# Order of VectorE's work in layer 0, PSUM banks in layer 1 and a longer lag in layer 2 of a four-layer graph attention kernel

## The chip, the core and the metric

The kernel runs on one core of a Trainium2 chip. The core has five engines that run at the same time, each with a queue of its own: TensorE (PE in the profile: matrix products and transposes), VectorE (DVE), ScalarE (ACT), GpSimd (POOL, here the issuer of all indirect gathers) and SyncE (SP, here an issuer of plain transfers). They wait for one another through semaphores. Products land in PSUM, which the kernel allocates in banks of 128 partitions by 512 floats; whoever wants a bank again waits until its last reader is done. The metric is the device time of one execution in microseconds; the median of three is taken.

## What is computed

A node matrix `x` (4096 x 256) passes four graph attention layers over one adjacency matrix `adj` (4096 x 4096, about nine neighbours a node, with the diagonal). Every layer normalises, clips at zero and adds its output to `x`:

```
h = maximum(layernorm(x), 0);  x = x + layer(h, adj)

layer 0: h = x @ W.T in 8 heads; logits = leaky(e_l[i] + e_r[j]) + gate * (|curv[i] - curv[j]| @ Wc.T)
         softmax over the neighbours j; out = attn @ h
layer 1: h = x @ W.T; e = leaky(a1.h[i] + a2.h[j]); out = softmax(e) @ h
layer 2: the same kind of e; out = elu(concat(softmax(e) @ x, -softmax(-e) @ x) @ wtrans)
layer 3: 4 heads; h = x @ W.T + b; score = leaky(h[i].h[j]), 1.0 where there is no edge
         out = relu(softmax(score) @ h)
```

Since the matrix is sparse, the kernel turns it into lists of edges first and then works on these.

## The kernel before

**Tiles and chunks.** The nodes are cut into 32 tiles of 128 rows (`NT`). The edges of a tile are packed into nine chunks (`EC`) of 128. For each chunk GpSimd issues one indirect DMA (L914) that fetches the rows of the neighbours from a table in device memory into a buffer `g`; there are six such buffers (`G`). The first seven chunks need rows below 3584 of the table only (28 tiles of 32); the last two may need any row. In layers 1 and 3 the ninth chunk is not gathered but expanded on TensorE (L1688, a product of a comparison matrix `to` with the table's last rows) and copied into `g` by ScalarE (L1692). That makes 9, 8, 9 and 8 gathers a tile in layers 0 to 3, 1088 in all.

**Who orders what.** TensorE runs in the order in which the program names its instructions (`manual_schedule`). The other engines' queues are ordered by a scheduler. `tc.issue_after(ins)` makes it put an instruction behind another of the same engine. `behind` is a dictionary of instructions to stand behind: `scores`, used in layers 1 and 2, puts its first addition (L1760) behind all that it holds.

**Layer 0** reads `adj`, finds each row's neighbours and works on the tiles, all at once. Its steps are put into a list `plan`, each with a due time in the plan's own units, and the program names them in the order of those times. Finding: `piece` and `pack` make keys (L1225), `rank` (L1229) picks the largest keys of a row with `nc.vector.max` (L1240) and `match_replace` (L1242), `columns` turns them into column numbers, `places` (L1365, its last operation at L1415) gives every edge its place, both for four tiles at once; `mark` (L897, L901) and `find_edges` make the numbers `nbr` (L1466) that the gathers take. Attention: `begin0` issues the gathers, `before0` (L1498, L1512) prepares, `score0` (L1505: `d`, the difference of the curvatures, then `e`), `turn_d`, `curve`, `weigh0` (L1531 multiplies the gathered rows by the weights), `attend0`, `finish0`, `turn1` and `rows1`, which makes the table of layer 1. The tile's work is centred on a time `w`, 22 units after its gathers are due; `score0` stands at `w - 9`. Tiles follow one another every 11.5 units.

**Layers 1 to 3** are driven by `run`. It takes a list of steps, each with a lag: in round r the step is called for tile r minus lag, and within a round steps are called in the order of the list. So in layer 1 TensorE meets, in round r: `go_to` of tile r+3 (L1674, a broadcast of column numbers that VectorE compares at L1677), `give2` of r-3, `attend1` of r-1, `turn2` of r-2, `before1` of r+1 (`give`, and the transposes of `s_chunks`), `rows2` of r-2 and `expand1` of r+1. `give` multiplies nine chunks into three small columns each (L908), which VectorE sums (L1752). Banks: `go_to` and `expand1` take turns in the one bank "pe" of the pool `ps_e`; `give` and `give2` in the one bank "pm" of `ps_m`.

In layer 2 the order on TensorE is `attend2` of r (L1894, 28 products), `turn3` of r-2 (L863, the transposes of the normed row `r`, L843), `turn_signed` of r-1 (L1916), `rows3` of r-2 (L872, which makes layer 3's table), `before2` of r+1 (L1641) and `through_wt` of r-1 (L1929). `finish2` (from L1937 on) makes `r` from the result of `through_wt`. Layer 3's first gathers wait until the rows of tile 27 are in its table.

Of the kernel before, what the change touches and what calls it, by code (L numbers as in the profile page):

```python
# [20 lines left out]
P = 128  # L21
C = 256
KC = C // P
H0, D0, CF = 8, 32, 6
# [672 lines left out]
EC = 9  # L697
# [16 lines left out]
def gnn_lists(  # L714
# [27 lines left out]
    nc = tc.nc  # L742
    N = x_in.shape[0]
    NT = N // P
# [77 lines left out]
    own = [const.tile([P, NT, 3], F32, name=f"own{i}") for i in (1, 2)]  # L822
# [8 lines left out]
    behind = {}  # L831
# [23 lines left out]
    def bank(pool, name, dtype=F32):  # L855
        t = pool.tile([P, 512], F32, name=name)
        return t if dtype == F32 else t.bitcast(dtype)
# [96 lines left out]
    with tc.tile_pool(name="keep", bufs=1) as keep, tc.tile_pool(  # L954
# [9 lines left out]
        g = g_pool.tile([P, EC + 1, ROW0], F32, name="g").rearrange("p c k -> p (c k)")  # L964
# [44 lines left out]
        for i, size in enumerate((0.5, 1.0)):  # L1009
            d = keep.tile([P, P], BF16, name=f"off_diag{i}")  # L1010
# [41 lines left out]
        at = keep.tile([P, NT], F32, name="at")  # L1052
# [176 lines left out]
        def rank(t):  # L1229

            r, i = divmod(t, RG // P)
            src = bank(ps_t, "pt")[:, : NH * KP]
            for h in range(NH):
                nc.tensor.transpose(
                    src[:, h * KP : (h + 1) * KP], key_t[r, h][:KP, i * P : (i + 1) * P], ident[:KP, :KP]
                )
            left = find.tile([P, NH * KP], F32, name="left", bufs=1)
            for a in range(0, KMAX, 8):
                best = keys[:, t, a : a + 8]
                nc.vector.max(out=best, in_=src)  # L1240
                if a + 8 < KMAX:
                    nc.vector.match_replace(out=left, in_to_replace=best, in_values=src, imm_value=-1.0)  # L1242
                    src = left
# [65 lines left out]
        lists = {}  # L1309
# [54 lines left out]
        def places(q, n):  # L1364


            s = slice(q, q + n)
            K = KMAX + KX
            is_, lasts, both = lists.pop(q)
            ps = bank(ps_t, "pt")[:, : 4 * n].rearrange("p (a t) -> p a t", a=4)  # L1370
            nc.tensor.matmul(ps[:, 0, :], lhsT=below, rhs=degree[:, s, 0], start=True, stop=True)
            nc.tensor.matmul(ps[:, 1, :], lhsT=up_to, rhs=degree[:, s, 1], start=True, stop=True)
            for i in range(2):
                nc.tensor.matmul(ps[:, 2 + i, :], lhsT=ones, rhs=degree[:, s, i], start=True, stop=True)

            def tmp(name, *shape):
                return find.tile([P, GT, *shape], F32, name=name, bufs=1)[:, :n]


            end, first, step = tmp("end"), tmp("first", 2), tmp("step", 2)  # L1380
            nc.vector.tensor_scalar(end, ps[:, 3, :], -1.0, float(HALF), op0=OP.mult, op1=OP.add)
            nc.vector.tensor_scalar(
                end, end, float(LATE * P - HALF), second, op0=OP.min, op1=OP.mult
            )
            nc.vector.scalar_tensor_tensor(
                at[:, s], ps[:, 0, :], room, end, op0=OP.add, op1=OP.add
            )
            nc.vector.tensor_scalar(at_late[:, s], ps[:, 1, :], float(HALF), None, op0=OP.add)
            nc.scalar.copy(of_tile[:, s, :], ps[:, 2:, :].rearrange("p a t -> p t a"))
            for i, a in enumerate((at, at_late)):  # L1390
                nc.vector.scalar_tensor_tensor(
                    minus[:, s, i], a[:, s], -2.0, degree[:, s, i], op0=OP.mult, op1=OP.subtract
                )


            nc.vector.tensor_sub(first[:, :, 0], at[:, s], lasts[:, :, 1])
            nc.vector.tensor_sub(step[:, :, 0], at_late[:, s], first[:, :, 0])
            nc.vector.tensor_sub(step[:, :, 1], lasts[:, :, 0], degree[:, s, 1])
            nc.vector.tensor_add(first[:, :, 1], at[:, s], step[:, :, 1])
            nc.vector.tensor_sub(step[:, :, 1], at_late[:, s], first[:, :, 1])  # L1400
            nc.vector.tensor_add(step[:, :, 1], step[:, :, 1], lasts[:, :, 1])
            place_, late = tmp("place_", K), is_[:, :, 1, :]
            for i, (a, b) in enumerate(((0, KMAX), (KMAX, K))):
                shape = [P, n, b - a]
                nc.vector.tensor_tensor(
                    late[:, :, a:b], late[:, :, a:b], step[:, :, i : i + 1].to_broadcast(shape),
                    op=OP.mult,
                )
                nc.vector.tensor_tensor(
                    place_[:, :, a:b], first[:, :, i : i + 1].to_broadcast(shape),  # L1410
                    slot[:, None, a:b].to_broadcast(shape), op=OP.add,
                )
            nc.vector.tensor_add(place_, place_, late)

            nc.vector.scalar_tensor_tensor(  # L1415
                both[:, :, 0, :], is_[:, :, 0, :], float(FAR), place_, op0=OP.mult, op1=OP.add
            )
            for i in range(n):
                of0[q + i]["list"] = both[:, i]

        def fits():

# [78 lines left out]
        def score0(t):  # L1501
            g = of0[t]["g"]
            pe = of0[t]["b"][:, : (EC + 1) * V0].rearrange("p (c k) -> p c k", c=EC + 1)
            d = of0[t]["d"] = work.tile([P, EC, CF], F32, name="d")
            nc.vector.tensor_sub(d, g[:, :EC, C + H0 :], pe[:, :EC, H0:])  # L1505
            e = of0[t]["e"] = work.tile([P, EC + 1, H0], F32, name="e")
            nc.vector.tensor_add(e, g[:, :, C : C + H0], pe[:, :, :H0])
            nc.vector.scalar_tensor_tensor(e, e, 0.2, e, op0=OP.mult, op1=OP.max)
# [65 lines left out]
        def at_piece(i):  # L1574
            return 8 + T_PIECE * min(i, FIRST) + T_LATER * max(i - FIRST, 0)
# [15 lines left out]
        for q, n in groups:  # L1591
            for t in range(q, q + n):
                last = at_piece((t // (RG // P) + 1) * per_r - 1) + 7 + 2.5 * (t % (RG // P))
# [6 lines left out]
        begun = {}  # L1600
# [3 lines left out]
            put(when, mark, t)  # L1604
            put(when + 4, find_edges, t)
        for t in range(NT):
            w = begun[t] + 22
            put(begun[t], begin0, t)
            put(max(begun[t] + 0.1, begun[0] + 12), begin0_late, t)
            put(w - 10, before0, t)  # L1610
            put(w - 9 + 0, score0, t)
            put(w - 7.8 + 0, turn_d, t)
            put(w + 2, curve, t)
            put(w + 3, weigh0, t)
            put(w + 15, attend0, t)
            put(w + 20, finish0, t)
            put(w + 24.6, turn1, t)
            put(w + 27, rows1, t)
        put(found[NT - 1] + 20, fits)
        for _, _, f, a in sorted(plan, key=lambda p: p[:2]):  # L1620
            f(*a)
        bad_1 = const.tile([P, 1], F32, name="bad_1")
        nc.vector.tensor_reduce(bad_1, bad, AX.X, OP.add)


    with tc.tile_pool(name="work", bufs=2) as work, tc.tile_pool(name="kept", bufs=1) as kept, tc.tile_pool(
# [36 lines left out]
        def keep_late(rows, width):  # L1663

            for b in range(0, LB, 2):
# [2 lines left out]
                rest = work.tile([P, 2, ROW1], F32, name="rest", bufs=1)[:, :n, :width]  # L1668
                in_parts([late_rows[:, b : b + n, i, :width] for i in range(3)], row, rest)

        def go_to(t, to):

            pm = bank(ps_e, "pe")[:, :P]
            nc.tensor.matmul(  # L1674
                pm, lhsT=col_late[:, t : t + 1].to_broadcast([P, P]), rhs=ident, start=True, stop=True
            )
            nc.vector.tensor_tensor(  # L1677
                to.rearrange("p (b e) -> p b e", b=LB), pm[:, None, :].to_broadcast([P, LB, P]),
                late_no[:, :, None].to_broadcast([P, LB, P]), op=OP.is_equal,
            )  # L1680
# [64 lines left out]

        a2_of = kept.tile([P, NT, EC + 1], F32, name="a2_of")

        def give(a, st, own_t):

            pe = bank(ps_m, "pm")[:, : EC * 3]  # L1750
            to_edges(pe.rearrange("p (c s) -> p c s", c=EC), st, upper(own_t))
            nc.vector.tensor_reduce(a[:, :EC], pe.rearrange("p (c s) -> p c s", c=EC), AX.X, OP.add)  # L1752
            nc.scalar.copy(a[:, SELF:], own_t[:, 0:1])
# [10 lines left out]
        with tc.tile_pool(name="l1_o", bufs=2, space=PSUM) as ps_o, tc.tile_pool(  # L1764
# [11 lines left out]

            def before1(t, of):
                a = of["a"] = work.tile([P, EC + 1], F32, name="a")
                give(a, of["st"], own[0][:, t, :])
                of["s"] = s_chunks(of["st"])  # L1780

            def give2(t, of):
                give(a2_of[:, t, :], of.pop("st"), own[1][:, t, :])

            def weigh1(t, of):
                s = scores(of["g"], of.pop("a"))
# [62 lines left out]
        with tc.tile_pool(name="l2_o", bufs=1, space=PSUM) as ps_o, tc.tile_pool(  # L1849
# [93 lines left out]

            rows3_of = []

            def turn3(t, of):
                of["hT"] = transposed(work, ps_t, of.pop("r"))

            def rows3(t, of):
# [19 lines left out]
                for k in range(K3):  # L1969
# [4 lines left out]
            run(  # L1974
                table2, ROW1, xs[1],
                [
                    (0, weigh2), (1, signed2), (2, finish2), (0, attend2), (2, turn3), (1, turn_signed),
                    (2, rows3), (-1, before2), (1, through_wt),
                ],
            )  # L1980

# [213 lines left out]
```

## Time and profile before

The time before is 1615.28 us, the median of three runs from 1614.99 to 1616.41. The execution that the profiler recorded is longer, 2272.3 us; all times below are of that one.

| stage | stretch, us | rounds | what bounds are in sight |
|---|---|---|---|
| up to the first gather | 0 to 108.4 | | reading `adj`, first lists |
| gathers of layer 0 | 108.4 to 753.6 | 32 tiles x 9 | |
| gathers of layer 1 | 780.1 to 1259.7 | 32 x 8 | TensorE busy 250.55 of 420 us |
| gathers of layer 2 | 1281.0 to 1724.3 | 32 x 9 | TensorE busy 349.52 of 440 us |
| gathers of layer 3 | 1766.3 to 2206.1 | 32 x 8 | TensorE busy 296.81 of 400 us |
| end | 2206.1 to 2272.3 | | last tiles |

The profile's page has a row of busy times by engine, then groups of equal instructions: engine, operation, output and input, how many, and behind the bar their busy time, the mean of one in ns, and how long the engine stood idle just before them, with the releaser of most of it. A line of the timeline reads: start, duration, engine, source line, operation, output and input, and in brackets the idle time before it and what ended it. A line of waits reads: who waited for whom, total us, times, longest. "issue" and "remote" name no instruction: the profile shows nothing, or something that it can't tell, as the releaser. The end of a product on TensorE is modelled.

### The profile page before, as it was taken

How to read it: one execution, taken by the hardware profiler on the slowest of the kernel's cores; microseconds unless marked ns; L12 is line 12 of the kernel's file. 1: busy time of each engine (PE TensorE's matmuls, PEld its weight loads, DVE VectorE, ACT ScalarE, POOL GpSimd, SP SyncE). 2: the span in 40 equal slices, each digit the busy share in tenths (PEclk: the TensorE clock that was granted, in tenths of full speed). 3: DMA queues.
4: the chain of work that ended last, by engine and by line, in shares of the span. 5: the costliest groups of instructions: out<-in, count | busy, mean ns of one | idle time of the engine just before them, and what ended most of it. 6: DMA issues, size and time to landing. Idle time of an engine off the chain costs nothing.

```text
span 2272.3 us, 28902 instructions
## 1 busy us (share of the span) xinstructions
PE 1431.2 (63%) x9569; PEld 1013.5 (45%) x9584; DVE 1100.3 (48%) x2979; ACT 765.2 (34%) x2246; POOL 1054.0 (46%) x1145
## 2 busy tenths in 40 slices
PE   5723745656646726656556637878889367767776
PEld 3412423333434414434444425666667345445544
DVE  5724635555543524434333323554555256666666
ACT  4623624454222322222222102333334143343343
POOL 2154243443344354454444455666562635565550
PEclk9855766666666857777777858999999778898888
DMA  8855555665333354444444444555554444455530
GB/s 284 267 187 172 187 172 180 212 212 163 83 88 99 88 164 130 128 124 129 130 133 131 140 138 122 158 161 157 155 156 139 129 134 147 149 157 154 161 107 21
DMA packets 167341, 338.02 MB, mean 149 GB/s; under 512 B 31760, under 2 KB 103696, under 8 KB 167184
## 3 DMA queue, kind: packets, MB, share of 16 engines
q0 software_dynamic: 52224, 145.30, 24.5%
q1 hardware_dynamic: 67714, 134.54, 18.1%
q10 hardware_dynamic: 47246, 56.27, 7.1%
q8 instruction: 77, 1.26, 0.2%
q14 instruction: 80, 0.66, 0.1%
HBM read 282.22 MB, written 53.77 MB: 148 GB/s over the span
## 4 chain that ended last, share of the span: by engine, by line
PE 25%; issue 12%; DVE 9%; another core or an unknown queue 8%; ACT 3%; POOL 1%; DMA 1%; DVEq 0%; ACTq 0%; POOLq 0%
PE o L934 5%; PE o L1894 4%; PE o L939 4%; PE pv L2025 3%; PE pt L872 3%; DVE v L2031 2%; PE pt L1929 2%; PE o L943 1%; POOL g L914 1%; DVE s L2052 1%; PE s_ps L1641 1%; DMA g<-table,nbr 1%; PE pe L1674 1%; DVE g L2064 1%
## 5 line engine op out<-in xcount | busy, mean ns | idle before, releaser
L914 POOL DMA_INDIRECT g<-table,nbr x1088 | 1037.8, 954 | 1065.1 <-issue 433.9
L1894 PE MATMUL o<-g,sw 128*128 128x257 f32 x896 | 206.0, 388 | 31.2 <-DVE sw L1872 23.6
L1894 PEld LDWEIGHTS o<-g,sw 128*128 128x128 f32 x896 | 173.1, 194 | 59.7 <-issue 25.3
L863 PE MATMUL pt<-ident,r 128*128 128x128 f32 x256 | 61.9, 328 | 193.4 <-DVE r L843 60.4
L2025 PE MATMUL pv<-parts,st 64*128 64x256 bf16 (+1 forms) x864 | 106.3, 308 | 97.8 <-DVE v L2031 42.0
L2031 DVE TENSOR_TENSOR v<-pv,g 128x512 f32<-128x512 f32 (+1 forms) x160 | 97.3, 634 | 89.6 <-remote 51.2
L863 PEld LDWEIGHTS pt<-ident,r 128*128 128x128 f32 x256 | 34.4, 162 | 219.2 <-issue 115.4
L1192 ACT ACTIVATE mask<-adj,minus_half 128x1024 bf16<-128x1024 int32 x112 | 125.2, 1141 | 18.1 <-issue 6.8
L934 PE MATMUL o<-g,sw 128*128 128x257 f32 (+1 forms) x320 | 125.5, 544 | 0.0
L865 ACT COPY hT<-pt 128x256 f32<-128x256 f32 x128 | 46.9, 367 | 233.4 <-PE pt L863 144.3
L872 PE MATMUL pt<-wcat,hT 128*128 128x272 f32 (+2 forms) x384 | 96.7, 371 | 45.3 <-ACT hT L865 32.4
L1674 PE MATMUL pe<-ident,col_late 128*128 128x128 f32 x64 | 23.3, 463 | 158.2 <-issue 144.8
L2025 PEld LDWEIGHTS <-st 64*128 64x128 bf16 (+1 forms) x864 | 61.4, 104 | 136.6 <-issue 125.9
L2081 ACT ACTIVATE y<-o,inv 128x64 f32<-128x64 f32 x128 | 36.0, 312 | 243.4 <-DVE inv L2077 143.5
L939 PE MATMUL o<-g,sw 128*64 128x257 f32 (+1 forms) x768 | 117.3, 448 | 0.0
L896 ACT ACTIVATE off<-place,minus 128x1152 bf16<-128x1152 f16 x64 | 80.0, 1250 | 58.1 <-DVE st L897 53.0
L1505 DVE TENSOR_TENSOR d<-g,pb 128x54 f32<-128x54 f32 x32 | 6.8, 211 | 180.1 <-remote 124.9
L934 PEld LDWEIGHTS o<-g,sw 128*128 128x128 f32 x320 | 85.8, 279 | 18.1 <-DVE g L2064 0.3
L872 PEld LDWEIGHTS pt<-wcat,hT 128*128 128x128 f32 x384 | 66.1, 208 | 60.2 <-ACT hT L865 36.5
L1531 DVE TENSOR_TENSOR g<-g,pb 128x2560 f32<-128x2560 f32 x32 | 90.1, 2816 | 4.7 <-ACT pb L1528 4.4
L1674 PEld LDWEIGHTS pe<-ident,col_late 128*128 128x128 f32 x64 | 14.7, 285 | 168.3 <-issue 153.1
L1688 PEld LDWEIGHTS <-st 128*128 128x128 bf16 x768 | 76.7, 105 | 19.4 <-issue 8.6
(363 smaller groups left out, 3028.5 us busy)
## 6 DMA issues: line engine op xcount, KB each, us to landing
adj<-in_adj_l SPq DMA_DIRECT2D x128, 512.0 KB
g<-table,nbr POOLq DMA_INDIRECT x1088
rows_of<-st ACTq DMA_DIRECT2D x16, 832.0 KB
st<-rows_of SPq DMA_DIRECT2D x16, 832.0 KB
x<-x SPq DMA_DIRECT2D x24, 512.0 KB
st<-rows_of SPq DMA_DIRECT2D x16, 576.0 KB
table<-row ACTq DMA_DIRECT2D x32, 258.0 KB
g<-table SPq DMA_DIRECT2D x64, 129.0 KB
```

The source lines that it names most:

```text
L863: nc.tensor.transpose(pt[:, k, :], h[:, k * P : (k + 1) * P], ident)
L872: nc.tensor.matmul(pp, lhsT=hT[:, k, :], rhs=w[:, k, :], start=(k == 0), stop=(k == KC - 1))
L896: nc.scalar.activation(off, place, AF.Abs, bias=minus[:, t, 0:1], scale=1.0)
L914: nc.gpsimd.indirect_dma_start(out=g[:, c, :width], out_offset=None, in_=table[: NE if c < EARLY else N, :], in_offset=bass.IndirectOffset ...
L934: nc.tensor.matmul(o, lhsT=a, rhs=b, start=(i == 0), stop=False)
L939: nc.tensor.matmul(o[rows], lhsT=s[:, c + h * HC, rows], rhs=g[:, c + h * HC, :width], start=False, stop=False,)
L1192: nc.scalar.activation(m, a, AF.Sign, bias=minus_half, scale=1.0)
L1531: nc.vector.tensor_mul(gh, gh, w[:, :, :, None].to_broadcast([P, K, H0, D0]))
L1688: nc.tensor.matmul(ps, lhsT=to[:, b * P : (b + 1) * P], rhs=late_rows[:, b, i, :width], start=(b == 0 and i == 0), stop=(b == LB - 1 and i ...
L1894: nc.tensor.matmul(o, lhsT=sw[:, h, i].rearrange("p s r -> p (s r)"), rhs=g[:, c, : C + 1], start=(i == 0), stop=(i == HC + 1),)
L2025: nc.tensor.matmul(to, lhsT=st[r, c * P : (c + 1) * P], rhs=parts[r, i, :], start=(i == 0), stop=(i == 2),)
L2031: nc.vector.tensor_mul(v[:, chunks, :], pv, g[:, chunks, :C])
```

## The change

It has three parts; no operation is added or taken away.

1. Layer 0. `behind["lists"]` holds the newest last step of `rank` or of `places`. For two of every four tiles (`t % 4 < 2`) `score0` puts its first operation, `d`, behind it in VectorE's queue. This is to let the finding of neighbours, which later gathers need, go ahead of scores whose own inputs may be late. The due time `w` gets a lower bound, which binds for tiles 0, 1 and 2 only (by 8, 4.5 and 1 units).
2. Layer 1. `go_to`, `give` and `give2` of a round share one bank "pm", in columns of their own; the bank "pe" is left to the expanded chunk. The comparison of the next round then has no need to wait for ScalarE's copy of that chunk.
3. Layer 2. `turn3` and `rows3` run three rounds after the tile's `attend2` instead of two (two still for tiles 30 and 31), and `turn3` is named ahead of `attend2`. The row that TensorE transposes is then one round older.

```diff
@@ rank
-                nc.vector.max(out=best, in_=src)
+                behind["lists"] = nc.vector.max(out=best, in_=src)
@@ places
-            nc.vector.scalar_tensor_tensor(
+            last = nc.vector.scalar_tensor_tensor(
                 both[:, :, 0, :], is_[:, :, 0, :], float(FAR), place_, op0=OP.mult, op1=OP.add
             )
...
+            behind["lists"] = last
@@ score0
-            nc.vector.tensor_sub(d, g[:, :EC, C + H0 :], pe[:, :EC, H0:])
+            with ExitStack() as queue:
+                if t < 32 and t % 4 < 2:
+                    queue.enter_context(tc.issue_after(behind["lists"].ins))
+                nc.vector.tensor_sub(d, g[:, :EC, C + H0 :], pe[:, :EC, H0:])
@@ the plan
-            w = begun[t] + 22
+            w = max(begun[t] + 22, begun[0] + 30 + 8 * t)
...
+        behind.pop("lists")
@@ go_to
-            pm = bank(ps_e, "pe")[:, :P]
+            round_[:] = [bank(ps_m, "pm")]
+            pm = round_[0][:, :P]
@@ give
-        def give(a, st, own_t):
-            pe = bank(ps_m, "pm")[:, : EC * 3]
+        def give(a, st, own_t, at):
+            pe = round_[0][:, at : at + EC * 3]
@@ before1, give2
-                give(a, of["st"], own[0][:, t, :])
+                give(a, of["st"], own[0][:, t, :], P)
-                give(a2_of[:, t, :], of.pop("st"), own[1][:, t, :])
+                give(a2_of[:, t, :], of.pop("st"), own[1][:, t, :], P + EC * 3)
@@ layer 2
+            def turn_lag(t):
+                return 3 if t < NT - 2 else 2
...
-                    (0, weigh2), (1, signed2), (2, finish2), (0, attend2), (2, turn3), (1, turn_signed),
-                    (2, rows3), (-1, before2), (1, through_wt),
+                    (0, weigh2), (1, signed2), (2, finish2), (turn_lag, turn3), (0, attend2),
+                    (1, turn_signed), (turn_lag, rows3), (-1, before2), (1, through_wt),
```

More of the change, by code (lines that the diff above doesn't have):

```diff
@@ L1669, in keep_late @@
                 in_parts([late_rows[:, b : b + n, i, :width] for i in range(3)], row, rest)
+        round_ = []
         def go_to(t, to):
-            pm = bank(ps_e, "pe")[:, :P]
+            round_[:] = [bank(ps_m, "pm")]
+            pm = round_[0][:, :P]
             nc.tensor.matmul(
```

## The prediction

> **What bounds the kernel now.** I read the page's busy row and its costliest group first, then each layer's window, then the waits, and last the moment at which one layer hands over to the next.
>
> ```profile
> PE 1431.2 (63%) x9569; PEld 1013.5 (45%) x9584; DVE 1100.3 (48%) x2979; ACT 765.2 (34%) x2246; POOL 1054.0 (46%) x1145
> L914 POOL DMA_INDIRECT g<-table,nbr x1088 | 1037.8, 954 | 1065.1 <-issue 433.9
> ```
>
> No engine is full. The gathers of GpSimd (POOL) come nearest to a floor: where nothing holds them, one starts 1.25 us after the last (0.95 busy, 0.30 idle), so 1088 of them fill 1088 x 1.25 = 1360 us, 11.25 us a tile in layers 0 and 2 (nine gathers) and 10.0 in layers 1 and 3 (eight). The first starts at 108.4 us of the profile and the last is followed by 66 us. Of 1065 us idle ahead of gathers 0.30 x 1088 = 326 is this spacing; the other 739 are stalls: about 285 in layer 0, 186 in layer 1, 105 in layer 2, 162 in layer 3, the handovers between layers included. But the profiled span is 2272.3 us and the timed run 1615.3. If spacing, start and tail hold in the timed run, only 1615 - 108 - 1360 - 66 = 81 us are left there for stalls, 11% of 739. So I price no profiled wait at its face value without asking what keeps it.
>
> ```profile
> 840.00:1260.00 420.00, 250.55 (x1808) 176.85 (x1809) 169.68 (x520) 104.54 (x279) 203.02 (x214) 0.74 0.46 135
> 1350.00:1790.00 440.00, 349.52 (x1704) 288.76 (x1702) 212.56 (x596) 144.34 (x589) 249.81 (x261) 0.91 0.52 150
> ```
>
> The columns are the stretch, then busy time of PE, weight loads, DVE, ACT and POOL, and the granted clock. Layer 2 (second line) has PE at 79% and is the one layer in which TensorE can bind; in layer 1 everything is loose.
>
> **What the Trainium skill says.** "Perfetto Trace Analysis", Tensor Engine Instruction (MATMUL, LD_WEIGHTS): the end of a matmul in a profile is estimated from its size, not seen. This trace agrees: in layer 1 the last product of L1688 ends by the model at 1045.32, and the copy that waits for it alone starts at 1051.51. The same page, GPSIMD Engine Instruction: time GpSimd by the spacing of starts; hence my 1.25 us. The same page, Matmuls: independent groups should rotate through PSUM banks, so that emptying one overlaps the next; in layer 1 the kernel before puts two unlike groups into one single bank. "TensorE: Matmul & The Clock Gate", Part 1: The HAM clock gate: the clock is halved after an idle window of about 3.4 us; the granted clock of 0.74 in layer 1 against 0.99 in the busy stretch 1730 to 1780 agrees. A PE that waits less also runs quicker, which I do not price apart.
>
> **Part 1, layer 0.** Nothing is computed more or less; d of two tiles in four is queued on VectorE behind the last rank step or behind the end of places. It bites once in the profile, at the start:
>
> ```profile
> 159.38 0.21 DVE L1505 TENSOR_TENSOR d<-g,pb 128x54 f32<-128x54 f32 x1 [40.32 <-remote]
> ...
> 168.79 2.82 DVE L1531 TENSOR_TENSOR g<-g,pb 128x2560 f32<-128x2560 f32 x1
> ...
> 180.06 2.81 DVE L1531 TENSOR_TENSOR g<-g,pb 128x2560 f32<-128x2560 f32 x1
> ...
> 184.99 0.17 DVE L1466 TENSOR_SCALAR nbr<-to_col 128x9 uint32<-128x9 f32 x1
> 185.43 0.94 POOL L914 DMA_INDIRECT g<-table,nbr  x1 [32.04 <-DVE nbr L1466]
> ```
>
> Tile 0's d holds VectorE for 40.3 us; behind it stand rank and key steps that were ready (159.51 to 163.1: 3.6 us), then the finding of tile 4's neighbours, which ends at 184.99 and lets tile 4's first gather go after an idle time of 32.0 us. In the queue order of the changed kernel the ranks and keys stand ahead of d, one of the two weighings (2.8 us) moves behind nbr of tile 4, and one marking (0.52 + 0.48 us, L897 and L901) moves ahead of it. Gain: 3.6 + 2.8 - 1.0 = 5.4 us. Lower end 0, if the 40 us are not VectorE's to win because d's own inputs are late anyway; upper end 32, all of that idle time. I take 5.4, as straight work off the queue. Later tiles: the waits of that layer's window are led by another cause (POOL on PE pb L1512, 141.8 us of 14), which the edit does not touch: 0. Queued behind the later d are the weighing and so attend of tile 0; they have six g buffers of slack, so 0. The shift of tiles 0 to 2 in the plan (8, 4.5 and 1 of its units) only orders the same work: 0.
>
> **Part 2, layer 1.** The column comparison (L1674) leaves the bank that the expanded chunk fills, and shares one with the two small products (give). What it removes:
>
> ```profile
> 1051.51 0.37 ACT L1692 COPY g<-pe 128x258 f32<-128x258 f32 x1 [5.22 <-remote]
> 1051.94 0.80 PE L1674 MATMUL pe<-ident,col_late 128*128 128x128 f32 x2 [6.62 <-issue]
> ...
> 1265.20 0.49 PE L1674 MATMUL pe<-ident,col_late 128*128 128x128 f32 x2 [0.46 <-ACT g L1692]
> ```
>
> Every round TensorE stands about 6.6 us in front of L1674 and starts 0.06 us after ScalarE's copy ends. While no gathers run (third line) the same wait is 0.46 us: the copy (0.37) and the passing on. So 6.6 is mostly the signal of L1688's real end, late under the profiler while GpSimd gathers; whoever waits for TensorE next will meet it. I take 0.46 x 27 rounds = 12.4 us as PE's true gain, and half of it, 6.2, as reaching the end, since gathers of 10.0 us a tile lie beside rounds of 6.4 to 7.4 us (the bursts after the last gather). Ends: 0 and the 138 us of the wait row of L1674. Added: PE's next L1674 now waits for VectorE's small sums (L1752) in the shared bank, done long before unless they are queued behind a score add (L1760) that waits for its gather: that row is 70.2 us in 13 times over 24 rounds, 2.9 a round. At the 11% above this is 0.32 x 27 = 9 us, which I leave to a rival.
>
> **Part 3, layer 2.** turn3 and rows3 run one round later, so PE no longer waits for the newest normed row. The three rows it can remove:
>
> ```profile
> PE pt L863 <- DVE r L843: 24.0, 11, 4.0
> PE pt L863 <- DVE s L1760: 20.1, 7, 4.1
> PE pt L863 <- DVE mv L841: 8.1, 3, 3.0
> ```
>
> They sum to 52 us. Ends: 11% of it (6) and all (52, though POOL's own wait for attend's buffers there is only 40.4, so 40 can reach the gathers). I take a quarter, 13 us, since PE's round without waits is 10.16 us against 11.25 of gathers: nearly balanced. Against it stands the handover to layer 3. Its first gathers need rows up to tile 27:
>
> ```profile
> 1752.92 6.23 PE L1894 MATMUL o<-g,sw 128*128 128x257 f32 x28
> 1763.09 6.23 PE L1894 MATMUL o<-g,sw 128*128 128x257 f32 x28
> 1766.33 0.94 POOL L914 DMA_INDIRECT g<-table,nbr  x1 [41.03 <-PE o L1894]
> ```
>
> POOL idles 41.0 us until PE has worked off its rounds; tile 27's rows leave in the second of these rounds, at about 1761. With a lag of three they leave one round later, and here PE runs without gaps at full clock, so the round costs 1763.09 - 1752.92 = 10.2 us. The shorter lag of tiles 30 and 31 comes after that and does not help it. Lower end 0, if PE has kept up and no backlog is left.
>
> **Sum.** 1615.3 - 5.4 - 6.2 - 13 + 10.2 = 1600.9, so 1601.
>
> **Rivals.** B, gathers bind and PE's waits are hidden: parts 2 and 3 bring nothing, layer 0 brings 5, half of the handover is lost: 1615 - 5 + 5 = 1615. For it speak the 81 us; against it, that POOL waits for PE at each handover. C, the profiled waits are real: 5.4 + 12.4 + 40.4 - 10.2 = 48 us, 1567. For it speaks that they come every round; against it, that they shrink to 0.46 us when gathering stops. D, slower: nothing is won in layer 2, the handover costs 10.2, and small sums behind late scores cost 9 with nothing hidden won in layer 1: 1615.3 - 5.4 + 10.2 + 9 = 1629 (1620 without the sums). For it speaks that the handover is a plain dependence on the path, in any state of the profiler; against it, that layer 2 has 28 rounds to earn it back.
>
> **Chances.** My case 0.46, B 0.20, C 0.16, D 0.18. Faster by over 0.2% (below 1612): mine, C and half of B, 0.72; within it: half of B, 0.10; slower: D, 0.18. The range runs from below C, 1562, to the middle of D, 1626, leaving out about 2 in 10.
>
> **What would show it.** Layer 0: tile 4's first gather earlier by some 5 us and no 40 us ahead of L1505. Layer 1: L1674 no longer behind L1692, and the long wait moved to another PE line or to ACT's copy; if the round shrinks by several us, C is right. Layer 2: the L863 rows gone and rounds under 13.9 us. Handover: the idle time ahead of layer 3's first gather longer by a round; if it is not, my loss is wrong. If L1674 shows waits for L1752, D is at work.

## The result, and the profile after

The changed kernel takes 1629.22 us (median of four, 1626.92 to 1630.86), the kernel before 1615.62 us (1614.99 to 1616.41): a ratio of 1.0083, 95% interval 1.0065 to 1.0100. It is 13.6 us slower, where I forecast 14 us faster.

One thing has to be known to read the numbers: the execution on which the prediction's profile rests took 2274 us, as the kernel before does on one of the four chips of this study (2275 us), while the times, and all profiles below unless said, come from chips on which it takes about 1615 us.

The page of the changed kernel, busy times and the gathers:

```profile
span 1628.0 us, 28958 instructions
PE 1262.6 (78%) x9584; PEld 926.6 (57%) x9584; DVE 1086.1 (67%) x2978; ACT 766.6 (47%) x2247; POOL 1062.9 (65%) x1145
L914 POOL DMA_INDIRECT g<-table,nbr x1088 | 1047.7, 963 | 415.8 <-issue 307.5
```

The idle time ahead of gathers is 415.8 us, not 1065.1; 0.30 x 1088 = 326 us of it is the spacing, over which nothing waits (the page puts 307.5 to no releaser, "issue"). To compare like with like I profiled the kernel before again on such a chip (first experiment below). From the starts of the gathers I took, for each stretch, what exceeds 1.25 us a gather; these are the stalls, in us:

| kernel | layer 0 | layer 1 | layer 2 | ahead of layer 3's first gather | layer 3 |
|---|---|---|---|---|---|
| before, second profile | 45.0 | 9.9 | 5.1 | 0.0 | 17.6 |
| changed | 45.5 | 9.1 | 5.0 | 15.7 | 18.1 |

With the handover from layer 0 to layer 1 (4.2 and 5.6) they come to 82 and 99 us. The loss is one number in one place. In layers 1 and 2 there was hardly a stall to win, and none was won. The timeline of GpSimd at that place, first of the kernel before (second profile), then of the changed kernel:

```profile
1213.48 0.95 POOL L914 DMA_INDIRECT g<-table,nbr  x1 [0.30 <-DVE x L1940]
1214.73 0.95 POOL L914 DMA_INDIRECT g<-table,nbr  x1 [0.30 <-issue]
```

```profile
1213.96 0.95 POOL L914 DMA_INDIRECT g<-table,nbr  x1 [0.31 <-issue]
1230.93 0.95 POOL L914 DMA_INDIRECT g<-table,nbr  x1 [16.02 <-DMA g<-table]
```

In both the first line is layer 2's last gather and the second layer 3's first. Before, it follows without a stall; after, it waits 16.02 us. The releaser that is named, the plain fetch of own rows, is a neighbour in time; by the program the gather needs the store of tile 27's rows (256 KB, with those of tile 26). The packets agree: in this profile the store's last one ends at 1229.59, 1.34 us ahead of the gather, and in the profiles of seven edits below the gather goes 1.26 to 1.53 us after it. When that row is made shows on TensorE, before (first) and after:

```profile
1198.71 6.23 PE L1894 MATMUL o<-g,sw 128*128 128x257 f32 x28
1207.46 1.13 PE L872 MATMUL pt<-w_s,hT 128*128 128x256 f32 x4 [1.86 <-ACT hT L865]
1211.14 6.23 PE L1894 MATMUL o<-g,sw 128*128 128x257 f32 x28
```

```profile
1199.76 6.23 PE L1902 MATMUL o<-g,sw 128*128 128x257 f32 x28
1206.26 1.03 PE L872 MATMUL pt<-w_s,hT 128*128 128x256 f32 x4
1211.77 3.78 PE L1937 MATMUL pt<-wt_s,two_t 128*128 128x256 f32 x8 [3.97 <-ACT two_t L1928]
1215.76 6.77 PE L1902 MATMUL o<-g,sw 128*128 128x257 f32 x28
1222.81 1.03 PE L872 MATMUL pt<-w_s,hT 128*128 128x256 f32 x4
```

Before, the product for tile 27 (L872 at 1207.46) stands in the round whose attend2 started at 1198.71. After, the product in that place is tile 26's (1206.26), and tile 27's comes at 1222.81, behind one more attend2. Between the two lie 16.6 us, not 10.2, and tile 27's product comes 15.4 us later than before. The chain of waits of the changed kernel tells why that round is long (start, us, what):

```profile
1206.29 2.45 DMA g<-table,nbr
1208.74 0.16 DVE s L1768
...
1210.38 0.24 DVE scale L1913
...
1211.77 3.78 PE pt L1937 x8
```

The score of a newer tile waits for its gather; the scale that TensorE's L1937 needs through ScalarE stands behind it in VectorE's queue. The round goes at the pace of the gathers, and after 3.97 us of idleness TensorE's products take longer (L1937 3.78 us, 1.98 in the round before; the granted clock is 0.78 from 1212 to 1223 us).

### The profile page after: what moved, and what is told of

Its sections match the earlier page's. It is cut to its first block, busy times and chain, and to the rows that moved or that the text cites. A ratio compares the mean times of both kernels' runs of the same rounds, so it can differ in the third digit from the quotient of the medians.

```text
span 1628.0 us, 28958 instructions
## 1 busy us (share of the span) xinstructions
PE 1262.6 (78%) x9584; PEld 926.6 (57%) x9584; DVE 1086.1 (67%) x2978; ACT 766.6 (47%) x2247; POOL 1062.9 (65%) x1145
## 3 DMA queue, kind: packets, MB, share of 16 engines
q8 instruction: 77, 1.26, 0.3%
## 4 chain that ended last, share of the span: by engine, by line
PE 47%; DVE 12%; POOL 10%; DMA 10%; issue 8%; ACT 6%; DVEq 0%; ACTq 0%; POOLq 0%; SPq 0%
PE o L1902 11%; POOL g L914 10%; DMA g<-table,nbr 10%; PE o L934 8%; PE o L939 7%; PE pt L1937 3%; PE pv L2037 3%; PE o L943 3%; PE pt L872 2%; DVE v L2043 2%; PE pe L1696 2%; PE s_ps L1646 2%; PE pt L863 1%; ACT mask L1192 1%; ACT s_f L1500 1%
## 5 line engine op out<-in xcount | busy, mean ns | idle before, releaser
L914 POOL DMA_INDIRECT g<-table,nbr x1088 | 1047.7, 963 | 415.8 <-issue 307.5
L1902 PEld LDWEIGHTS o<-g,sw 128*128 128x128 f32 x896 | 169.5, 192 | 63.3 <-DVE sw L1880 38.1
L2037 PE MATMUL pv<-parts,st 64*128 64x256 bf16 (+1 forms) x864 | 93.1, 287 | 79.9 <-DVE v L2043 77.9
L872 PE MATMUL pt<-wcat,hT 128*128 128x272 f32 (+2 forms) x384 | 94.8, 365 | 7.9 <-ACT hT L865 5.7
L939 PE MATMUL o<-g,sw 128*64 128x257 f32 (+1 forms) x768 | 100.3, 397 | 0.0
L1646 PE MATMUL s_ps<-ident_b,st 128*128 128x128 bf16 x864 | 67.8, 227 | 38.9 <-DVE sw L1798 38.9
L863 PE MATMUL pt<-ident,r 128*128 128x128 f32 x256 | 57.3, 310 | 48.8 <-DVE r L843 23.2
L2076 DVE TENSOR_TENSOR g<-g,pm 128x2048 f32<-128x2048 f32 x32 | 73.2, 2289 | 25.8 <-ACT pm L2069 25.8
L934 PE MATMUL o<-g,sw 128*128 128x257 f32 (+1 forms) x320 | 89.5, 413 | 0.0
L1696 PEld LDWEIGHTS <-st 128*128 128x128 bf16 x768 | 78.9, 107 | 14.1 <-issue 1.6
L1646 PEld LDWEIGHTS <-st 128*128 128x128 bf16 x864 | 56.9, 101 | 49.1 <-DVE sw L1798 39.9
L2064 DVE TENSOR_REDUCE s<-v 128x36 f32<-128x2304 f32 x32 | 81.7, 2553 | 1.1
L1500 ACT CAST s_f<-pt 128x1024 f32<-128x1024 bf16 x64 | 37.7, 641 | 92.7 <-PE o L943 92.7
L872 PEld LDWEIGHTS pt<-wcat,hT 128*128 128x128 f32 x384 | 65.5, 205 | 22.0 <-ACT hT L865 9.6
```

The lines of the kernel that those rows point to most:

```text
L872: nc.tensor.matmul(pp, lhsT=hT[:, k, :], rhs=w[:, k, :], start=(k == 0), stop=(k == KC - 1))
L914: nc.gpsimd.indirect_dma_start(out=g[:, c, :width], out_offset=None, in_=table[: NE if c < EARLY else N, :], in_offset=bass.IndirectOffset ...
L934: nc.tensor.matmul(o, lhsT=a, rhs=b, start=(i == 0), stop=False)
L939: nc.tensor.matmul(o[rows], lhsT=s[:, c + h * HC, rows], rhs=g[:, c + h * HC, :width], start=False, stop=False,)
L1646: nc.tensor.transpose(pt[:, c, :], st[:, c * P : (c + 1) * P], ident_b)
L1696: nc.tensor.matmul(ps, lhsT=to[:, b * P : (b + 1) * P], rhs=late_rows[:, b, i, :width], start=(b == 0 and i == 0), stop=(b == LB - 1 and i ...
```

## Experiments

**The kernel before, profiled again** (no edit).

> The kernel before once more, for a second profile: the first one's span is 2272.3 us against 1615 timed, that of the changed kernel 1628.0 against 1629. If the stretch was the profiler's, this one has a span near 1615 and stalls ahead of gathers (beyond 1.25 us a gather) of about 1615 - 108 - 1360 - 60 = 85 us instead of 739; it then shows at which handover or layer the changed kernel loses 13.6 us. If the long waits belong to the kernel before, the span is near 2270 again.

Its span is 1610.0 us, its stalls add up to 82 us. The long waits do not belong to the kernel but to the execution that the first profile caught, most likely to its chip: on the chip of 2275 us a profile shows them again (last experiment). Which chip the first profile came from is not on record. How the layer 1 wait looks here, TensorE and ScalarE in one round:

```profile
705.85 2.74 PE L1688 MATMUL pe<-late_rows,st 128*128 128x258 bf16 x12
708.63 0.37 ACT L1692 COPY g<-pe 128x258 f32<-128x258 f32 x1 [1.99 <-DMA g<-table,nbr]
709.06 0.50 PE L1674 MATMUL pe<-ident,col_late 128*128 128x128 f32 x2 [0.46 <-ACT g L1692]
```

The product ends at 708.59 and its copy starts 0.04 us later, with gathers running beside it, where the first profile had 6.2 us between them. In 24 of layer 1's 32 rounds this distance is 0.03 to 0.05 us. So the 6.2 us, which I took for the real end of the product that the profile can't see, are no error of the modelled end here. The wait of L1674 is 0.46 us.

**The three parts alone**, each on the kernel before with the edits of the diff above that belong to it.

> Part 1 alone (d queued behind the lists, and the due times of tiles 0 to 2). Theory H (the loss is the handover from layer 2 to layer 3): 1610 to 1616, no loss. Rival Q (the queueing in layer 0 holds up scores and so the buffers of gathers): 1625 or more, with the loss between the first gathers and the end of layer 0.

> Part 2 alone (comparison and small products of layer 1 in one bank). Theory H: 1609 to 1616. Rival M (the small sums hold the shared bank behind late scores): 1620 or more, with stalls of gathers inside layer 1.

> Part 3 alone (later products in layer 2). Theory H: 1622 to 1632, with the idle time of GpSimd ahead of layer 3's first gather one TensorE round (about 10 us) longer than in the kernel before and the gathers of layer 2 no sooner done. Rivals Q and M: 1603 to 1616.

Measured beside the kernel before (median 1614.7):

| part | time | ratio, 95% interval | stall ahead of layer 3 |
|---|---|---|---|
| 1, layer 0 | 1614.23 | 0.9993 (0.9978 to 1.0008) | 0.3 |
| 2, bank | 1614.97 | 0.9999 (0.9989 to 1.0009) | 1.7 |
| 3, lag | 1627.43 | 1.0080 (1.0060 to 1.0099) | 14.1 |

Part 3 has all of the loss, at the handover; parts 1 and 2 can't be told from nothing, and both intervals leave out the gains that I forecast for them (5.4 us is 0.9967, 6.2 us 0.9962). What part 2 did with its wait shows in the waits of layer 1 (560 to 840 us), before (second profile) and changed:

```profile
PE pe L1674 <- ACT g L1692: 15.5, 28, 1.0
```

```profile
PE pm L908 <- DVE st L1685: 20.3, 26, 0.8
PE pm L908 <- DVE a_of L1760: 11.5, 3, 5.1
```

The wait for ScalarE's copy is gone, 15.5 us in 28 rounds. In its place the small products wait for VectorE's comparison in the bank that they now share, 20.3 us in 26; part 2 alone shows the same row with the same numbers. The wait was moved, not removed; and neither reaches the end, since the stalls of layer 1's gathers are 9.9 and 9.1 us.

Part 1 did what it is for: before, tile 4's first gather stands 2.40 us for its list (first line, GpSimd, second profile); in the changed kernel the gather in that place, the 37th, goes on time. The 40.3 us that VectorE stood at tile 0's `d` in the first profile are 6.05 in the second.

```profile
158.38 0.94 POOL L914 DMA_INDIRECT g<-table,nbr  x1 [2.40 <-DVE nbr L1466]
```

In part 1 alone layer 0's stalls are 41.4 us against 45.0, in the whole change 45.5. Over all profiles from chips of 1615 us they are 44.6 to 47.9 in the nine without part 1, 41.4 to 45.5 in the four with it, some 3 us less by the means; but the handover to layer 1 has 3.9 to 4.3 without and 5.3 to 5.6 with it. Half of the little that was won is lost there, and the rest is below what the times can tell.

**Tile 27 alone a round late.** On the kernel before, one tile:

```diff
+            def turn_lag(t):
+                return 3 if t == 27 else 2
-                    ... (0, attend2), (2, turn3), (1, turn_signed), (2, rows3), ...
+                    ... (0, attend2), (turn_lag, turn3), (1, turn_signed), (turn_lag, rows3), ...
```

> The kernel before with one edit: turn3 and rows3 of tile 27 alone run one round later, after attend2 as before; all other tiles keep the lag of two. Theory H: the whole loss is there, 1624 to 1632, with 14 to 17 us of idle time ahead of layer 3's first gather. Rival R: 1613 to 1617.

1621.59 us, ratio 1.0045 (1.0030 to 1.0060), 7.3 us: the handover is confirmed as a place of loss, but it is little more than half of part 3's 12.9 us. One tile out of 32 costs it. I had expected the whole loss here.

**A lag of four.** Part 3 alone with `4 if t < 28 else 3 if t < 30 else 2`.

> Part 3 alone with a lag of four (three for tiles 28 and 29, two for 30 and 31). Theory H: tile 27's row comes two rounds later than in the kernel before; a round of TensorE after the last gathers is 10.2 us, so 10 more than part 3 alone: 1635 to 1642. Rival R gives a loss that doubles with the rounds inside layer 2: stalls of gathers within layer 2 of over 15 us in place of 4.

1634.94 us, at the lower edge of what was expected, ratio 1.0125 (1.0099 to 1.0152), 20 us; the stall ahead of layer 3 is 19.2 us, those inside layer 2 stay at 5.0. The loss grows with the lag, and only at the handover.

**The lag ended early, order unchanged.** The whole change with `3 if t < 24 else 2`.

> The whole change, but with the lag of three in layer 2 only for tiles 0 to 23, two from tile 24 on. Theory H (the loss is tile 27's row one round later): the idle time ahead of layer 3's first gather falls from 17 us to under 2, and the time to 1611 to 1617. Rival R (the longer lag costs in every round of layer 2, by later work queued on VectorE and ScalarE): 1620 to 1629.

A miss: 1631.16 us, ratio 1.0102 (1.0080 to 1.0125), with 22.3 us of stall ahead of layer 3. TensorE in one of the last rounds:

```profile
1221.51 0.66 PE L863 MATMUL pt<-ident,r 128*128 128x128 f32 x2 [4.04 <-DVE r L843]
1221.96 8.86 PE L1902 MATMUL o<-g,sw 128*128 128x257 f32 x28
```

With a lag of two, turn3 ahead of attend2 needs the row that the round before has just begun to make: TensorE stands 4.04 us, and the attend2 that follows takes 8.86 us instead of 6.23. (The Trainium skill's "TensorE: Matmul & The Clock Gate", Part 1: The HAM clock gate, has the clock halve after some 3.4 us of idleness and come back after as long a busy stretch; this fits: the granted clock is 0.69 from 1222.0 to 1230.6 us, and 1.00 over an attend2 of 6.23 us in the changed kernel, 1226 to 1232 us.) Such rounds take about 17 us, and tile 27's row is later than with the lag of three. So lag and order go together, and the short lag needs the old place:

```diff
+                    ... (early_lag, turn3_early), (0, attend2), (2, turn3_late), (1, turn_signed), (early_lag, rows3), ...
```

where `early_lag` is 3 for tiles 0 to 23 and 2 after, `turn3_early` acts on the former and `turn3_late` on the latter.

> The whole change, but from tile 24 of layer 2 on lag and place of turn3 and rows3 are those of the kernel before; once more, for a chip on which the kernel before takes about 1615 us. Theory H' (the loss is when tile 27's row leaves, lag and order together): under 2 us of stall ahead of layer 3's first gather, 1611 to 1617. Rival R (something else of the change costs): 1622 or more.

1614.47 us, ratio 0.9992 (0.9979 to 1.0004), 2.6 us of stall, a little over the 2 expected. All of the change but the end of layer 2 costs nothing, and brings nothing that can be measured: no version here that computes the same beats the kernel before.

**The load beside the store.** What makes part 3 cost 12.9 us where tile 27 alone costs 7.3? In the timeline of the changed kernel, the queues of SyncE and ScalarE (load of edge marks, store of tile 27's rows), then the first gather:

```profile
1224.37 0.32 SPq L1717 DMA_DIRECT2D st<-rows_of  x1
1224.39 0.41 ACTq L774 DMA_DIRECT2D table<-row  x1
1230.93 0.95 POOL L914 DMA_INDIRECT g<-table,nbr  x1 [16.02 <-DMA g<-table]
```

A load of 832 KB for layer 3's tiles 6 and 7 is issued 0.02 us ahead of the store, and the gather goes 6.5 us after the store. With tile 27 alone late the store is issued first, by 0.84 us, and the gather follows 3.1 us after it (1222.12, 1225.22). The load was put behind the fetch of some tile's own rows in SyncE's queue:

```diff
+            own_row[t] = nc.sync.dma_start(g[:, SELF, :width], tile_rows(table, t))
...
+            if expand and t == 6:
+                queue.enter_context(tc.issue_after(own_row[0].ins))
```

> Part 3 alone with the 832 KB load for layer 3's tiles 6 and 7 queued behind the fetch of tile 0's own rows. Theory C (that load beside the store makes the store land 3 us later): stall ahead of layer 3's first gather 11 to 12 us in place of 14.7, time 1622 to 1626. Rival: stall 14 to 16, 1625 to 1631.

That run told nothing: tile 0's rows had been fetched long before, so the load still started 0.02 us ahead of the store (1222.35, 1222.37); 1628.89 us, ratio 1.0089 (1.0063 to 1.0114), stall 13.2 us. With `own_row[5]`, which waits for the last attend2, it does move:

> Part 3 alone with the 832 KB load for layer 3's tiles 6 and 7 queued behind the fetch of tile 5's own rows, so that it starts after the store of tile 27's rows has landed. Theory C (that load makes the store land 3 us later): the store lands 2 to 3 us after its issue, stall ahead of layer 3's first gather 11 to 12 us in place of 14.7, time 1622 to 1626. Rival (the landing is as slow without it): stall 14 to 16, 1625 to 1631.

1621.81 us, ratio 1.0046 (1.0031 to 1.0060), stall 9.4 us, both slightly under what was expected. The three lines of this run:

```profile
1220.28 0.37 ACTq L774 DMA_DIRECT2D table<-row  x1
1228.73 0.43 SPq L1714 DMA_DIRECT2D st<-rows_of  x1
1223.32 1.17 POOL L914 DMA_INDIRECT g<-table,nbr  x1 [9.60 <-DVE low L1942]
```

The gather goes 3.0 us after the store, and the whole of part 3 now costs 7.4 us, as tile 27 alone does. The edit also moves four fetches of own rows, which had stood behind the load in SyncE's queue (1223.3 to 1225.5 in the run before), ahead of the store, so the load is not yet shown to be the cause. The packets of the transfers decide: in the changed kernel the load's 128 packets run from 1225.33 to 1229.03 and the store's 256 from 1227.66 to 1229.59, while the fetches begin only at 1229.18; with the load behind tile 5 the store's run from 1221.16 to 1222.06. The load holds the store back.

So part 3's loss is about 7.4 us for the round and 5.5 us (1.0080 less 1.0046, of 1614; by the intervals give or take 4) for the load. The stalls of the two profiles differ by 4.7 us (14.1 and 9.4): 3.4 is the landing, the rest that the store itself is issued sooner, of which I know only that attend2 ahead of it took 6.23 us and not 7.20.

**Gathers eased.** Does part 3 take anything away at all? In this experiment, in layer 2, two of nine chunks are filled by plain transfers of SyncE with the table's first tile (layer 2 then computes on other rows), so that gathers need 8.75 us a tile; with the old order, and with the early lag up to tile 23 and the old order after it.

```diff
+            if fewer and c in (3, 4):
+                nc.sync.dma_start(g[:, c, :width], tile_rows(table, 0))
+                continue
```

> The kernel before with seven gathers of nine in layer 2, the other two chunks filled by plain transfers with the table's first tile (so layer 2 computes on other rows); 8.75 us of gathers a tile. Theory G (gathers set layer 2's pace): the pace becomes TensorE's, 10.2 to 11 us a tile, and the time falls by 15 to 40 us. Rival (TensorE sets it already): no faster than 1610.

> The same with turn3 ahead of attend2 and the lag of three for tiles 0 to 23. Theory G: layer 2 at 10.2 us a tile or less, and faster than seven gathers with the old order by as much as that one's rounds are longer than 10.2 us; if those are 10.2 already, no difference. Rival (part 3 takes nothing away on such a chip): within 3 us.

1607.56 us (0.9939, 0.9918 to 0.9960) and 1603.26 us (0.9913, 0.9889 to 0.9937). The first gathers of two neighbouring tiles late in layer 2, old order and then early lag:

```profile
1145.53 0.94 POOL L919 DMA_INDIRECT g<-table,nbr  x1 [1.52 <-PE pt L863]
1155.70 0.94 POOL L919 DMA_INDIRECT g<-table,nbr  x1 [1.73 <-PE pt L863]
```

```profile
1141.54 0.94 POOL L919 DMA_INDIRECT g<-table,nbr  x1 [1.70 <-PE o L1899]
1151.45 0.94 POOL L919 DMA_INDIRECT g<-table,nbr  x1 [1.46 <-PE o L1899]
```

From the tenth tile on GpSimd now waits for TensorE in every tile, and a round takes 10.17 us; with part 3 9.91. From layer 2's first gather to layer 3's it is 350.8 us and 345.3. So part 3 does shorten TensorE's round, by a quarter of a microsecond. The two times differ by less than their intervals.

With nine gathers the same quarter is there, but it buys nothing. TensorE starts layer 2 behind the gathers (the first attend2 at 904 us, the first gather at 850) and has a backlog to work off, at 10.16 us a round before, at 9.91 in the changed kernel. Two rounds next to each other, before (second profile) and changed:

```profile
1153.83 1.13 PE L872 MATMUL pt<-w_s,hT 128*128 128x256 f32 x4
1163.99 1.13 PE L872 MATMUL pt<-w_s,hT 128*128 128x256 f32 x4
```

```profile
1150.87 1.03 PE L872 MATMUL pt<-w_s,hT 128*128 128x256 f32 x4
1160.78 1.03 PE L872 MATMUL pt<-w_s,hT 128*128 128x256 f32 x4
```

Among layer 2's waits (880 to 1180 us) one row of the kernel before is gone in the changed one, and it has this size a round:

```profile
PEld pt L872 <- ACT hT L865: 6.6, 25, 0.3
```

Since gathers need 11.25 us a tile, TensorE has caught up three rounds before the end in the kernel before and some eight in the changed one; from there it goes at the pace of the gathers, and the gain is gone.

With seven gathers the old order gained only 9 us from 64 gathers fewer, where 15 to 40 were expected, since TensorE, now 39 us behind at the end, kept layer 3 waiting instead (38.62 us ahead of its first gather).

**On a chip of 2275 us.** Four kernels had run first on a chip where the kernel before takes 2275.06 us. The profile of the first of them has 721 us of stalls, against 739 in the profile of the prediction.

> The whole change, but in layer 2 only tiles 0 to 23 have turn3 ahead of attend2 and the lag of three; from tile 24 on lag and place are those of the kernel before (in the run that ended the lag early, turn3 stayed ahead of attend2 and TensorE stood 4 us a round for the normed row). Theory H' (the loss is when tile 27's row leaves, lag and order together): under 2 us of stall ahead of layer 3's first gather, 1611 to 1617. Rival R (something else of the change in layer 2 or before it costs): 1622 or more.

> Part 3 alone, with the 832 KB load of edge marks for layer 3's tiles 6 and 7 queued on SyncE behind the fetch of tile 0's own rows, so that it can't start in the same moment as the store of tile 27's rows. Theory C (the store landed 5 us after its issue in place of 2 to 4 because this load ran beside it): the stall ahead of layer 3's first gather is 3 us shorter than part 3 alone (11 to 12 in place of 14.7), the time 1622 to 1626. Rival (the landing is as slow without it): stall 14 to 16, 1625 to 1631.

> The kernel before, where in layer 2 two of nine chunks are not gathered but filled with the table's first tile by plain transfers of SyncE (so layer 2 computes on other rows): gathers then need 8.75 us a tile. Theory G (gathers set layer 2's pace and hide what part 3 takes away): layer 2 now runs at the pace of TensorE with its waits, 10.5 to 12 us a tile, and the time falls by 64 x 1.25 = 80 us at most. Rival (TensorE sets the pace already): 11.2 us a tile as before.

> The same seven gathers in layer 2, with the lag of three and turn3 ahead of attend2 for tiles 0 to 23 as the whole change has it, the tail as before. Theory G: the waits that part 3 takes away now count, the round falls to about 10.2 us, and the run is 5 to 25 us faster than seven gathers with the old order. Rival: within 3 us of it.

Their expectations were written for 1615 us and can't be judged. The ratios: 0.9951 (0.9928 to 0.9975) for the whole change with the old order at the end, 0.9977 (0.9949 to 1.0005) for part 3 with the load queued behind tile 0's rows, 0.9769 and 0.9727 for the two with seven gathers. On that chip the change without its late tail is 11 us faster; the L863 waits for L843 fall from 24.0 us in 11 to 3.7 in one. So without its late tail the change gains there somewhat under half of the 24.6 us that I had added up from a profile like this one, and nothing on the chips of 1615 us. The change as it stands did not run on that chip, and which of its parts brings the 11 us was not separated.

## Why the prediction was wrong

- **The floor was right.** 1.25 us a gather and 81 us left for stalls in the timed run: the second profile has 82. The conclusion was not drawn. Of the 28 us between forecast and result, 24.6 are three gains that did not come, and the rest is the handover. The step that failed is the overlap: having found that 11% of the stalls could be left, I still let half of what TensorE gains in layer 1 and a quarter of its waits in layer 2 reach the end. Gathers of 10.0 and 11.25 us a tile hide both (stalls of 9.9 and 9.1 us in layer 1, 5.1 and 5.0 in layer 2, before and changed).
- **Part 1, 5.4 us.** The direction holds (the wait for tile 4's list is gone), but 2.4 us were there to win (the spacing included), not the 32 of the first profile; the time moved by 0.9993, which is not told from 1.
- **Part 2, 6.2 us: the term that failed in layer 1.** The size per round, 0.46 us, was right. "Half of it, as reaching the end" was wrong, it is none; and the new wait in the shared bank came from the comparison L1685, not from the sums alone that I named. It is larger than the one removed (20.3 against 15.5 us).
- **Part 3's gain, 13 us: the term that failed in layer 2.** The three L863 rows do not appear in layer 2's waits of the second profile (880 to 1180 us). What the part takes away is 0.25 us a round, another wait (L872 for ScalarE's copy), and with nine gathers a tile nothing of it reaches the end.
- **The handover, 10.2 us.** The mechanism, tile 27's row one round later on the path to layer 3, is what the change costs. The size was too small, by 3 us net: part 3 costs 12.9, about 7.4 for the round and 5.5 for a load that came to start with the store, which I had not seen. The reason given, that TensorE still works off a backlog at 10.2 us a round, was wrong for these rounds: the backlog is used up by then, and the round before tile 27's row is longer because it waits for gathers (12.5 us even in the kernel before, 1194.97 to 1207.46). With tile 27 alone late its product comes 13.0 us later than before (1220.46) and the stall is 9.7. The difference is slack of about 0.9 us, by estimate (before, the store's last packet ends at 1212.47 and the gather goes at 1214.73, where 1.3 us between them are enough), a quicker landing (last packet 1.8 us after the issue in place of 3.3), and gathers that were due 0.8 us later.
- **Rival D** gives 1629, the measured time, but the sum is right by luck: its 5.4 us from layer 0 did not come, and its 9 us for small sums in layer 1 did not either (stalls 9.9 and 9.1). Its first half, "the handover is a plain dependence on the path", is what was right. Rival B was right on layers 1 and 2 and wrong to halve the handover.

## What to carry to other kernels

Compare the profiled span with the timed run before pricing a wait: when the span is 40% longer, the floor says how much of all stalls can be left in the timed run, and a wait above that can't be priced from such a profile. A longer software lag is paid once, at the end of the loop, by whoever waits for its last rows; shorten it for the last tile that the next layer needs, and then put the step back to the place where its input is ready. A freed bank or wait only counts if its engine sets the pace; look for where the wait went.

## What the hardware showed that I had not expected

- The same program takes about 1615 us on three chips and 2275 us on a fourth. In the first profile, which looks like one of the latter, a copy that waits for a product mostly starts 6.2 us after the modelled end while gathers run (mostly 3.4 to 6.3 us in the whole change with the old order at the end, profiled on the fourth chip); in the second profile mostly 0.04 us. Why is open.
- A 256 KB store that is issued 0.02 us after an 832 KB load released its reader 6.5 us after its issue, in three runs; where no packets of SyncE's transfers ran beside its own, 3.0 to 3.6 us, in four others. In the run with the old order at the end on a chip of 1615 us it took 7.4 us: there packets of `x` and of own rows ran beside it.
- In the run that ended the lag early, after waits of 3.7 to 4.3 us the 28 products of attend2 take 8.3 to 8.9 us in place of 6.23, so a wait of 4 us costs TensorE 6.2 to 6.7. With tile 27 alone late a wait of 3.0 us was enough for eight products behind it (L1929) to take 3.37 us in place of 1.95.
